# A GRU network and graph attention: the last three pairs get an attention schedule of their own

## The chip, the cores and the metric

The kernel runs on one core of a Trainium2 chip. Its time is device microseconds of one execution; each kernel is run several times and the median is given. A core has TensorE (PE, matrix products and transposes into PSUM), VectorE (DVE), ScalarE (ACT, table functions and copies), GpSimd (POOL) and SyncE (SP), which issues the transfers here. The engines run side by side, each works through its own instructions in order, and semaphores tie them together.

## The reference

There are 64 graphs with 256 nodes and 256 features. Layer 0 is three rounds of a gated recurrent unit (GRU) over the adjacency matrix, layer 1 is graph attention; each adds its input and normalises.

```python
def gru(inp, h):
    gi, gh = inp @ w_ih.T + b_ih, h @ w_hh.T + b_hh        # 3 parts each: r, z, n
    r, z = sigmoid(i_r + h_r), sigmoid(i_z + h_z)
    n = tanh(i_n + r * h_n)
    return (1 - z) * n + z * h
h = x
for i in range(3):
    m = h @ weight[i]
    h = gru(einsum('bst,bsd->btd', adj != 0, m), h)
v = layernorm(x + h)
Wh = v @ W;  s1, s2 = Wh @ a[:256], Wh @ a[256:]
e = leaky_relu(s1[:, :, None] + s2[:, None, :], 0.2)
attn = softmax(where(adj > 0, e, -9e15), axis=2)
out = layernorm(v + attn @ Wh)
```

## The kernel before

The graphs are worked off in 32 pairs (`NP`), numbered 0 to 31. A pair has four blocks of 128 nodes (`K`), two to a graph (`C`). A GRU round of a pair is a *block* `(p, i)`, pair and layer. The blocks go in diagonals, so that three pairs are under way at a time: (p, 0), (p-1, 1), (p-2, 2). The list therefore ends with (29,2), (31,1), (30,2), (31,2), each a GRU round, and after a pair's third round comes its attention.

The order of the work is written out by hand. A clock counts *ticks*; `at(t, step)` puts a step on a heap, and `tick()` inside a block's products (line 468 and 473) runs the steps that are due. A block has 12 ticks. What a step issues stands, on every engine's queue, behind all that was issued before it. When the blocks are all issued, the loop of line 788 runs the remaining steps in the order of their ticks, with no products between them.

A GRU round keeps its state transposed, `hT` (features on partitions, 512 nodes of the pair on the free axis). A 32-bit product is built of three pieces of each operand, `hH`, `hL`, `hD` and `aH`, `aL`, `aD` (line 465). PE writes banks of PSUM, ACT and DVE empty them (lines 470 to 474), ACT computes sigmoid and tanh (483), POOL multiplies and adds (491 to 501), DVE forms the new `hT` (504).

Attention of pair p, whose clock starts at t, the end of its third block (`attention`, line 543), in the kernel before, by ticks from t:

- +7, +13: x, transposed, comes back from DRAM (`vT <- xT`, line 550), and `hT` is added to it.
- +24, +29, +32: v is turned to node-major order by the DMA's transpose, which works on 16-bit halves: two transposes (line 296), four gathers (302), and on ACT four copies that join the halves (286).
- +34, +36: statistics of the first layer norm (DVE), power (POOL).
- +37 to +41: projection with W and both score vectors (PE, line 586), scaling (595, 597); the adjacency matrix is loaded again and made into a mask (622).
- +42 to +47: score rows turned by PE (605), leaky scores (ACT, 609), masking (DVE, 628), maxima (630), exponentials with their sums (ACT, 633).
- +50 to +57: the weights are turned: for pairs 0 to 29 by two DMA transposes, eight gathers and four joins (655, 302, 670), for pairs 30 and 31 by PE and a DVE copy (648, 701).
- +58 (+54 for the last two) on: combination `po` (PE, 680), division and residual (DVE, 691), second layer norm (DVE, POOL, and ACT in line 531), store (706).

With T for the tick at which block (29,2) ends, the three last blocks take T to T+12, to T+24 and to T+36; pair 29 has t = T, pair 30 t = T+24, pair 31 t = T+36.

`room` (line 264) says where the tiles of attention lie: pairs 0 to 29 in a pool of their own (`late`), 30 and 31 in buffers of the GRU pieces, which are free by then.

Of the kernel before, what the change touches and what calls it, by code (L numbers as in the profile page):

```python
# [9 lines left out]
F32 = mybir.dt.float32  # L10
F32R = mybir.dt.float32r
U8 = mybir.dt.uint8
# [15 lines left out]
def kernel(  # L28
# [37 lines left out]
    nc = tc.nc  # L66
    B, N, D = x.shape
    L = weight.shape[0]
    C = N // P
    G = 2  # L70
# [18 lines left out]
    def at(t, step):  # L89
        clock[1] += 1  # L90
        heappush(pending, (t, clock[1], step))
# [14 lines left out]
    def bank(name):  # L106
        return psum.tile([P, 512], F32, tag="bank", name=name)
# [255 lines left out]
    def from_T(hT, d):  # L363
        pt = bank("pt")
        for k in range(K):
            nc.tensor.transpose(pt[:, k * P:(k + 1) * P], hT[:, d, k * P:(k + 1) * P], ident)  # L366
        return pt
# [174 lines left out]

    def attention(p, t):
# [97 lines left out]
            nc.vector.reciprocal(s.sm, s.sm)  # L641
        at(t + 51, divide)

        def weights_T(g):
            pts[g] = bank("pt")
            for j in range(C):
                for c in range(C):
                    nc.tensor.transpose(pts[g][:, (j * C + c) * P:(j * C + c + 1) * P],
                                        s.sc[:, g * C + c, j * P:(j + 1) * P], ident)
# [13 lines left out]
        def gather_weights(g):  # L663
            gather(planes(g), s.eT[:, g].rearrange("p c j n -> p (c j n)").bitcast(U16).rearrange(
                "p (m b n) -> p m b n", b=2, n=P))

        def join_weights(g):
            dst = s.eT[:, g].rearrange("p c j n -> p (c j n)").bitcast(U16).rearrange("p (n h) -> p h n", h=2)
            for h in (1, 0):
                ENGINES[("aa", "aa")[g][1 - h]](dst[:, h], planes(g)[:, h].rearrange("p m n -> p (m n)"))  # L670

        def combine(g):
            pts[g] = bank("po")
            for c in range(C):
                for j in range(C):
                    if by_dma:
                        e = s.eT[:, g, c, j, :]
                    else:
                        e = s.sc[:, g * C + j, c * P:(c + 1) * P]
                    nc.tensor.matmul(pts[g][:, c * D:(c + 1) * D], e, s.wh[:, g, j, :],  # L680
                                     start=(j == 0), stop=(j == C - 1))

        def add(g):

            if by_dma:
                s.o = s.eT.rearrange("p g c j n -> p g c (j n)")
            else:
                s.o = s.v
            for c in range(C):
                k = g * C + c  # L690
                nc.vector.scalar_tensor_tensor(s.o[:, g, c, :], pts[g][:, c * D:(c + 1) * D], s.sm[:, k:k + 1],
                                               s.v[:, g, c, :], op0=ALU.mult, op1=ALU.add)
        by_dma = p < NP - 2
        for g in range(G):
            if by_dma:
# [3 lines left out]
            else:  # L699
                at(t + 51 + g, lambda g=g: weights_T(g))  # L700
                at(t + 52 + g, lambda g=g: nc.vector.tensor_copy(flat(s.sc[:, g * C:(g + 1) * C, :]), pts[g]))
            at(t + (58 if by_dma else 54) + g, lambda g=g: combine(g))
            at(t + (58 if by_dma else 54) + 1 + g, lambda g=g: add(g))
# [4 lines left out]
        at(t + 60, lambda: layer_norm(s.o, f"b_{p}", (t + 60 + 1, t + 64, t + 66, t + 71), s.eps, store))  # L708


    CLOSE = (5, 5, 5, 7, 8, 8), (6, 6, 7)
# [50 lines left out]
    for n, (p, i) in enumerate(blocks):  # L762
        if n + 1 < len(blocks):
            np_, ni = blocks[n + 1]
            if ni == 0:
                if np_ < FROM:
                    after(1, lambda p=np_: begin(p))
                after(1, lambda p=np_: take_x(p))
                after(2, lambda p=np_: ones(p))
                nxt = np_ + 1  # L770
                if nxt < FROM:
                    after(7, lambda p=nxt: load_x(p))
                elif nxt < NP:
                    later = {}
                    after(26, lambda p=nxt, d=later: d.update(f=x_turned(p)))
                    after(30, lambda d=later: d["f"]())
                    after(33, lambda p=nxt: x_joined(p))
                    after(33, lambda p=nxt: load_x(p))
                after(5 if nxt < FROM else 34, lambda p=nxt: load_adj(p))
            front(np_, ni, clock[0],   # L780
                  CLOSE if n and np_ == blocks[n - 1][0] else
                  EARLY if np_ < FROM and not ni else (FIRST, SECOND, THIRD)[ni])
        gates(p, i, (2, 3, 5) if n + 2 >= len(blocks) or blocks[n + 2][0] == p else (2, 5, 9))
        if i == L - 1:
            attention(p, clock[0])
        elif FROM <= p and p + i + 1 < NP:
            h_turned(p, i, clock[0])
    while pending:
# [31 lines left out]
```

## Time and profile before

| | us |
|---|---|
| median of 3 runs (2116.19 to 2118.03) | 2117.34 |
| the profiled execution | 2112.89 |
| its span (first to last instruction) | 2111.1 |
| PE busy | 2053.3 (97%) |
| DVE, ACT, POOL busy | 1769.4, 1659.1, 1611.8 |
| mean granted clock of PE | 0.988 |

The page has a table of busy time by engine, the span in 40 slices, the transfers, the chain of work that ended last (followed back from the last instruction to whatever released each step) and the groups of instructions. Beside it the trace can be asked for the busy time of each engine in any stretch, and for each engine's instructions in order, with the idle time ahead of each and what ended it. The start of one instruction to the start of the next is what it costs on its engine; the durations given overlap by some 0.1 us on DVE and ACT, and on PE by more.

### The profile page before, as it was taken

Reading aid. Unit: us, or ns where it says so; the run is one execution under the profiler, and the core shown is the slowest. Engines: PE = TensorE matmul, PEld = TensorE weight load, DVE = VectorE, ACT = ScalarE, POOL = GpSimd, SP = SyncE. Lnnn points to the kernel's source line nnn. Section 1 sums busy time; section 2 is a strip of 40 time slices with the busy share of each in tenths; the row PEclk is TensorE's granted clock in tenths of the full one; section 3 lists DMA queues with packets and bytes.
Section 4 is the critical chain, followed back from the end, with each engine's and each line's share of the span. In section 5 each row is a group of like instructions: output and inputs, shape, how many; then the busy total and the mean of one; then the engine's idle time right before and its main releaser. Section 6 shows DMA issues by size and latency. Waiting matters only on the chain.

```text
span 2111.1 us, 31355 instructions
## 1 busy us (share of the span) xinstructions
PE 2053.3 (97%) x9860; PEld 1726.3 (82%) x9860; DVE 1769.4 (84%) x2863; ACT 1659.1 (79%) x3020; POOL 1611.8 (76%) x1114
## 2 busy tenths in 40 slices
PE   8999999999999999999999999999999999999965
PEld 5788888888888888888888888888888888888854
DVE  5666778899898899998899989888999889998765
ACT  4566788788888888888888888888888888888754
POOL 6778677777787887787888778788778788877641
PEclk9999999999999999999999999999999999999987
DMA  4111234666566666566666566666656656654333
GB/s 130 31 41 41 71 89 111 150 131 127 133 140 136 144 126 145 124 134 139 133 150 130 128 132 140 133 148 121 151 122 135 138 134 150 130 129 92 71 88 82
DMA packets 545509, 252.17 MB, mean 119 GB/s; under 512 B 370432, under 2 KB 537088, under 8 KB 545344
## 3 DMA queue, kind: packets, MB, share of 16 engines
q1 hardware_dynamic: 543552, 248.34, 53.2%
q8 instruction: 78, 1.28, 0.3%
q10 hardware_dynamic: 1616, 1.57, 0.2%
q14 instruction: 87, 0.71, 0.1%
q0 software_dynamic: 176, 0.27, 0.1%
HBM read 69.74 MB, written 33.55 MB: 49 GB/s over the span
## 4 chain that ended last, share of the span: by engine, by line
PE 93%; DVE 2%; POOL 2%; DMA 1%; ACT 1%; SPq 1%; issue 0%; POOLq 0%; ACTq 0%; DVEq 0%
PE pga L465 48%; PE pgb L465 24%; PE pa L436 8%; PE po L680 5%; PE pwh L586 5%; PE s L605 1%; PE pt L366 1%; SPq L302 1%; DMA rows_hH<-in_L_gnn_w_hh_dram 0%; DMA v<-vT 0%; POOL t L491 0%; POOL n L501 0%; DMA second<-v 0%; POOL t L492 0%; PE pw L238 0%
## 5 line engine op out<-in xcount | busy, mean ns | idle before, releaser
L491 POOL TENSOR_TENSOR t<-hT,n 128x512 f32<-128x512 f32 x192 | 264.2, 1376 | 186.2 <-ACT n L483 186.0
L501 POOL TENSOR_TENSOR n<-n,t 128x512 f32<-128x512 f32 x192 | 287.4, 1497 | 117.8 <-DVE t L474 113.7
L497 POOL TENSOR_TENSOR n<-n,r 128x512 f32<-128x512 f32 x192 | 316.1, 1646 | 73.6 <-ACT r L483 48.5
L465 PE MATMUL pga<-hH,whhH_whh 128*128 128x512 f32 x1152 | 370.6, 403 | 0.0
L465 PE MATMUL pgb<-hD,whhD_whh 128*128 128x512 f32 x1152 | 357.1, 391 | 1.4 <-DVE hD L138 1.4
L465 PE MATMUL pga<-hL,whhL_whh 128*128 128x512 f32 x1152 | 356.8, 391 | 0.3 <-POOL hL L135 0.3
L492 POOL TENSOR_TENSOR t<-t,z 128x512 f32<-128x512 f32 x192 | 271.0, 1411 | 15.0
L135 POOL TENSOR_TENSOR hL<-hT,hH 128x1024 fp32r<-128x1024 f32 x96 | 258.3, 2691 | 10.6 <-ACT hH L132 10.5
L465 PEld LDWEIGHTS pgb<-hD,whhD_whh 128*128 128x128 f32 x1152 | 216.2, 188 | 49.1 <-DVE hD L138 1.7
L465 PEld LDWEIGHTS pga<-hL,whhL_whh 128*128 128x128 f32 x1152 | 216.4, 188 | 47.8 <-POOL hL L135 0.8
L465 PEld LDWEIGHTS pga<-hH,whhH_whh 128*128 128x128 f32 x1152 | 207.9, 189 | 34.3
L138 DVE SCALAR_TENSOR_TENSOR hD<-hH,hT 128x1024 fp32r<-128x1024 f32 x96 | 202.4, 2109 | 0.0
L470 ACT ACTIVATE r<-pga 128x512 f32<-128x512 f32 x192 | 114.0, 594 | 109.1 <-PE pga L465 75.9
L483 ACT ACTIVATE n<-n,bi 128x512 f32<-128x512 f32 x192 | 138.9, 723 | 75.5 <-POOL n L501 75.4
L436 PE MATMUL pa<-A,hi 128*128 128x256 f32 x768 | 193.6, 285 | 0.2 <-DVE A L377 0.2
L504 DVE TENSOR_TENSOR hT<-t,n 128x512 f32<-128x512 f32 x192 | 187.6, 977 | 5.9 <-POOL t L492 5.9
L436 PE MATMUL pa<-A,lo 128*128 128x256 f32 x768 | 192.1, 283 | 0.0
L474 DVE SCALAR_TENSOR_TENSOR r<-pgb,r 128x512 f32<-128x512 f32 x192 | 132.0, 688 | 69.0 <-PE pgb L465 44.3
L135 DVE TENSOR_TENSOR aL<-pa,aH 128x512 fp32r<-128x512 f32 x192 | 131.1, 683 | 63.8 <-ACT aH L132 63.7
L132 ACT ACTIVATE aH<-pa 128x512 fp32r<-128x512 f32 x192 | 115.9, 604 | 64.0 <-PE pa L436 64.0
L470 ACT ACTIVATE t<-pga 128x512 f32<-128x512 f32 x192 | 115.3, 601 | 59.2 <-PE pga L465 54.3
L483 ACT ACTIVATE z<-z,b_sum 128x512 f32<-128x512 f32 x192 | 140.7, 733 | 18.9 <-DVE z L474 18.1
(147 smaller groups left out, 5391.1 us busy)
## 6 DMA issues: line engine op xcount, KB each, us to landing
adj<-in_adj_dram SPq DMA_DIRECT2D x64, 512.0 KB, 3.8
second_h<-first_h SPq DMA_DIRECT2D x204, 128.0 KB, 4.0
x<-in_x_dram SPq DMA_DIRECT2D x32, 512.0 KB, 3.8
xT<-hT SPq DMA_DIRECT2D x32, 512.0 KB, 4.5
vT<-xT SPq DMA_DIRECT2D x32, 512.0 KB, 3.3
second<-v SPq DMA_DIRECT2D x128, 128.0 KB, 3.6
sc<-eT SPq DMA_DIRECT2D x240, 64.0 KB, 2.2
out_dram<-eT SPq DMA_DIRECT2D x30, 512.0 KB, 4.3
```

The lines of the kernel that those rows point to most:

```text
L135: eng.tensor_sub(dst, src, hi.bitcast(F32))
L138: nc.vector.scalar_tensor_tensor(dst, hi.bitcast(F32), 1.0 + U, src, op0=ALU.mult, op1=ALU.subtract)
L436: nc.tensor.matmul(pt[:, g * N:(g + 1) * N], h[:, g * C + c, :], s.A[:, g, c, :], start=(n == 0), stop=(n == len(todo) - 1))
L465: nc.tensor.matmul(pt, w[:, d, o * P:(o + 1) * P], m[:, d, :], start=n in (0, ends + 1), stop=n in (ends, len(todo) - 1))
L470: nc.scalar.activation(dst, a, AF.Copy, scale=1.0 + U)
L474: nc.vector.scalar_tensor_tensor(dst, b, -1.0 / U, dst, op0=ALU.mult, op1=ALU.add)
L483: nc.scalar.activation(dst, dst, func, bias=bias)
L491: nc.gpsimd.tensor_sub(t, h, n)
L492: nc.gpsimd.tensor_mul(t, t, z)
L497: after(2, lambda r=r, n=n: nc.gpsimd.tensor_mul(n, n, r))
L501: after(1, lambda n=n, t=t: nc.gpsimd.tensor_add(n, n, t))
L504: after(lags[2], lambda n=n, t=t, h=h: nc.vector.tensor_add(h, t, n))
```

## The change

The last three pairs, 29 to 31, get a function of their own, `attention_last`. In it v and the weights are turned by PE (transposes into PSUM, then copies by ACT and DVE); masks, masking, maxima, exponentials, division and the steps after them are made graph by graph; the addition to `vT` is split in two; scaling goes to ACT for odd node blocks and to DVE for even ones (before: first two ACT, last two DVE). Each of the three pairs has a timetable (`LAST`, ticks from its t), with shorter distances than before. Tiles of pair 29 move, `vT` apart: v to the place of x, wh to that of A, the weights to that of hT. The path of the last two pairs in `attention` goes away.

```diff
-        if p < NP - 2:
+        if p < NP - 3 or p == NP - 3 and kind == "vT":
             return late.tile(shape, F32, tag=kind, name=name, bufs=2 if kind == "v" else 1)
+        if p == NP - 3:
+            pool, tag, bufs = {"v": (io, "x", 1), "wh": (work, "A", 3), "sc": (work, "hT", 4)}[kind]
+            return pool.tile(shape, F32, tag=tag, name=name, bufs=bufs)
         tag = {"v": "hH", "vT": "hD", "wh": "aH", "sc": "aD"}[kind]
...
-        by_dma = p < NP - 2
         for g in range(G):
-            if by_dma:
-                at(t + 50 + g, lambda g=g: turn_weights(g))
-                at(t + 52 + g, lambda g=g: gather_weights(g))
-                at(t + 56 + g, lambda g=g: join_weights(g))
-            else:
-                at(t + 51 + g, lambda g=g: weights_T(g))
-                at(t + 52 + g, lambda g=g: nc.vector.tensor_copy(flat(s.sc[:, g * C:(g + 1) * C, :]), pts[g]))
...
+    def attention_last(p, t, T):
+        s = pairs[p]
+        pts = {}
+        each = lambda step, dt, every=1, n=G: [at(t + dt + every * g, lambda g=g: step(g)) for g in range(n)]
...
+        def sum_(d):
+            nc.vector.tensor_add(s.vT[:, d, :], s.vT[:, d, :], s.hT[:, d, :])
+
+        def turn(d):
+            if d == 0:
+                s.v = room("v", [P, G, C, D], p)
+            pts["v", d] = from_T(s.vT, d)
+
+        def turned(d):
+            evacuate(nodes(s.v, d), pts["v", d].rearrange("p (k n) -> p k n", k=K))
...
+        def spread(k):
+            rs = s.rs[:, k:k + 1]
+            for dst, src in ((s.s1[:, k:k + 1], pts[k][:, D:D + 1]),
+                             (s.s2[:, k, :], pts[k][:, D + 1:D + 2].to_broadcast([P, P])),
+                             (s.wh[:, k // C, k % C, :], pts[k][:, :D])):
+                if k % 2:
+                    nc.scalar.activation(dst, src, AF.Copy, scale=rs)
+                else:
+                    nc.vector.tensor_scalar(dst, src, rs, None, op0=ALU.mult)
+
+        def rows(g):
+            pts["s2", g] = bank("s2")
+            for c in range(C):
+                nc.tensor.transpose(pts["s2", g][:, c * P:(c + 1) * P], s.s2[:, g * C + c, :], ident)
...
+        def exps(g):
+            for k in range(g * C, (g + 1) * C):
+                nc.scalar.activation(s.sc[:, k, :], s.sc[:, k, :], AF.Exp, bias=s.nm[:, k:k + 1],
+                                     accum_out=s.sm[:, k:k + 1])
...
+        def weights_T(g):
+            pts["w", g] = bank("pt")
+            for j in range(C):
+                for c in range(C):
+                    nc.tensor.transpose(pts["w", g][:, (j * C + c) * P:(j * C + c + 1) * P],
+                                        s.sc[:, g * C + c, j * P:(j + 1) * P], ident)
+
+        def weights(g):
+            for j in range(C):
+                nc_copy = ENGINES["av"[j]]
+                nc_copy(s.sc[:, g * C + j, :], pts["w", g][:, j * N:(j + 1) * N])
...
+        at(t + T["again"], again)
+        each(sum_, T["add"])
+        at(t + T["adja"], adj_again)
+        each(turn, T["turn"])
+        each(turned, T["turn"] + 1)
+        at(t + T["st"], norm)
+        each(project, T["proj"], 1, K)
+        each(spread, T["spr"], 1, K)
+        each(rows, T["rows"], T["e_rows"])
+        each(mask, T["mask"], T["e_mask"])
+        each(scores, T["sco"], T["e_sco"])
+        each(masked, T["mskd"], T["e_mskd"])
+        each(top, T["max"], T["e_max"])
+        each(exps, T["exp"], T["e_exp"])
+        each(divide, T["div"], 1)
+        each(weights_T, T["wT"], T["e_wT"])
+        each(weights, T["wc"], T["e_wc"])
+        each(combine, T["comb"], T["e_comb"])
+        each(add, T["res"], T["e_res"])
+        at(t + T["l2"], norm_last)
...
+    LAST = (
+        dict(again=5, add=10, adja=8, turn=13, st=15, pw=17, proj=17, spr=19, rows=22, mask=18, sco=22, mskd=24, max=27, exp=28, div=30, wT=30, wc=30, comb=31, res=32, l2=32, l2p=34, l2s=37, l2a=39, e_rows=1, e_mask=1, e_sco=1, e_mskd=1, e_max=1, e_exp=1, e_wT=1, e_wc=1, e_comb=1, e_res=1),
+        dict(again=5, add=9, adja=8, turn=12, st=15, pw=17, proj=12, spr=20, rows=22, mask=16, sco=22, mskd=24, max=24, exp=26, div=28, wT=27, wc=28, comb=30, res=31, l2=31, l2p=34, l2s=35, l2a=38, e_rows=1, e_mask=1, e_sco=1, e_mskd=1, e_max=1, e_exp=1, e_wT=1, e_wc=1, e_comb=1, e_res=1),
+        dict(again=4, add=6, adja=11, turn=6, st=10, pw=12, proj=9, spr=15, rows=17, mask=15, sco=17, mskd=18, max=19, exp=21, div=22, wT=21, wc=22, comb=24, res=25, l2=25, l2p=28, l2s=29, l2a=31, e_rows=1, e_mask=1, e_sco=1, e_mskd=1, e_max=1, e_exp=1, e_wT=1, e_wc=1, e_comb=1, e_res=1),
+    )
...
         if i == L - 1:
-            attention(p, clock[0])
+            if p < NP - len(LAST):
+                attention(p, clock[0])
+            else:
+                attention_last(p, clock[0], LAST[p - NP])
```

The steps that are left out here (`again`, `norm`, `project`, `scores`, `mask`, `masked`, `top`, `divide`, `combine`, `add`, `store`) issue what their namesakes in `attention` issue, for one graph or one node block at a time.

More of the change, by code (lines that the diff above doesn't have):

```diff
@@ L642, in attention @@
         at(t + 51, divide)
[L644 to L649, printed above, removed]
         def turn_weights(g):
@@ L675, in combine @@
                 for j in range(C):
-                    if by_dma:
-                        e = s.eT[:, g, c, j, :]
-                    else:
-                        e = s.sc[:, g * C + j, c * P:(c + 1) * P]
+                    e = s.eT[:, g, c, j, :]
                     nc.tensor.matmul(pts[g][:, c * D:(c + 1) * D], e, s.wh[:, g, j, :],
@@ L683, in add @@
         def add(g):
[L685 to L688, printed above, removed]
+            s.o = s.eT.rearrange("p g c j n -> p g c (j n)")
             for c in range(C):
@@ L692, in add @@
                                                s.v[:, g, c, :], op0=ALU.mult, op1=ALU.add)
-        by_dma = p < NP - 2
         for g in range(G):
-            if by_dma:
-                at(t + 50 + g, lambda g=g: turn_weights(g))
-                at(t + 52 + g, lambda g=g: gather_weights(g))
-                at(t + 56 + g, lambda g=g: join_weights(g))
-            else:
-                at(t + 51 + g, lambda g=g: weights_T(g))
-                at(t + 52 + g, lambda g=g: nc.vector.tensor_copy(flat(s.sc[:, g * C:(g + 1) * C, :]), pts[g]))
-            at(t + (58 if by_dma else 54) + g, lambda g=g: combine(g))
-            at(t + (58 if by_dma else 54) + 1 + g, lambda g=g: add(g))
+            at(t + 50 + g, lambda g=g: turn_weights(g))
+            at(t + 52 + g, lambda g=g: gather_weights(g))
+            at(t + 56 + g, lambda g=g: join_weights(g))
+            at(t + 58 + g, lambda g=g: combine(g))
+            at(t + 59 + g, lambda g=g: add(g))
         def store():
@@ L708, in attention, with again, norm, adj_again @@
         at(t + 60, lambda: layer_norm(s.o, f"b_{p}", (t + 60 + 1, t + 64, t + 66, t + 71), s.eps, store))
+    def attention_last(p, t, T):
+        s = pairs[p]
+        pts = {}
+        each = lambda step, dt, every=1, n=G: [at(t + dt + every * g, lambda g=g: step(g)) for g in range(n)]
+        def again():
+            s.vT = room("vT", [P, C, GN], p)
+            nc.sync.dma_start(s.vT, s.far)
+        def sum_(d):
[6 more added lines that the diff above has]
+            evacuate(nodes(s.v, d), pts["v", d].rearrange("p (k n) -> p k n", k=K))
+        def norm():
+            s.rs, s.eps = layer_norm(s.v, f"a_{p}", (t + T["st"], t + T["pw"]))
+        def adj_again():
+            load_adj(p)
+        def project(k):
+            if k == 0:
+                s.wh = room("wh", [P, G, C, D], p)
+                s.sc = room("sc", [P, K, N], p)
+                s.s1 = work.tile([P, K], F32, tag="s1", name=f"s1_{p}")
+                s.s2 = s.sc[:, :, :P]
+                s.nm = work.tile([P, K], F32, tag="nm", name=f"nm_{p}")
+                s.sm = work.tile([P, K], F32, tag="sm", name=f"sm_{p}")
+            pts[k] = bank("pwh")
+            for d in range(C):
+                nc.tensor.matmul(pts[k][:, :D + 2], s.vT[:, d, k * P:(k + 1) * P], gw[:, d, :],
+                                 start=(d == 0), stop=(d == C - 1))
+        def spread(k):
[11 more added lines that the diff above has]
+                nc.tensor.transpose(pts["s2", g][:, c * P:(c + 1) * P], s.s2[:, g * C + c, :], ident)
+        def scores(g):
+            for k in range(g * C, (g + 1) * C):
+                nc.scalar.activation(s.sc[:, k, :], pts["s2", g][:, :N], AF.Prelu,
+                                     bias=s.s1[:, k:k + 1], alpha=ALPHA)
+        def mask(g):
+            if g == 0:
+                s.adj = loaded_adj.pop(p).rearrange("p g c n -> p g (c n)")
+                s.mask = work.tile([P, K, N], U8, tag="mask", name=f"mask_{p}", bufs=1)
+            nc.vector.tensor_scalar(flat(s.mask[:, g * C:(g + 1) * C, :]), s.adj[:, g], 0.0, None, op0=ALU.is_le)
+        def masked(g):
+            ks = slice(g * C, (g + 1) * C)
+            nc.vector.copy_predicated(flat(s.sc[:, ks, :]), flat(s.mask[:, ks, :]), neg.to_broadcast([P, C * N]))
+        def top(g):
+            ks = slice(g * C, (g + 1) * C)
+            nc.vector.tensor_reduce(s.nm[:, ks], s.sc[:, ks, :], AX.X, ALU.max, negate=True)
+        def exps(g):
+            for k in range(g * C, (g + 1) * C):
+                nc.scalar.activation(s.sc[:, k, :], s.sc[:, k, :], AF.Exp, bias=s.nm[:, k:k + 1],
+                                     accum_out=s.sm[:, k:k + 1])
+        def divide(g):
+            ks = slice(g * C, (g + 1) * C)
+            nc.vector.tensor_mul(s.sm[:, ks], s.sm[:, ks], s.rs[:, ks])
+            nc.vector.reciprocal(s.sm[:, ks], s.sm[:, ks])
+        def weights_T(g):
[8 more added lines that the diff above has]
+                nc_copy(s.sc[:, g * C + j, :], pts["w", g][:, j * N:(j + 1) * N])
+        def combine(g):
+            pts["o", g] = bank("po")
+            for c in range(C):
+                for j in range(C):
+                    nc.tensor.matmul(pts["o", g][:, c * D:(c + 1) * D], s.sc[:, g * C + j, c * P:(c + 1) * P],
+                                     s.wh[:, g, j, :], start=(j == 0), stop=(j == C - 1))
+        def add(g):
+            for c in range(C):
+                k = g * C + c
+                nc.vector.scalar_tensor_tensor(s.v[:, g, c, :], pts["o", g][:, c * D:(c + 1) * D],
+                                               s.sm[:, k:k + 1], s.v[:, g, c, :], op0=ALU.mult, op1=ALU.add)
+        def norm_last():
+            layer_norm(s.v, f"b_{p}", (t + T["l2"], t + T["l2p"], t + T["l2s"], t + T["l2a"]), s.eps, store)
+        def store():
+            nc.sync.dma_start(out[p * G:(p + 1) * G].rearrange("g (c p) d -> p g c d", p=P), s.v)
+        at(t + T["again"], again)
[18 more added lines that the diff above has]
+        at(t + T["l2"], norm_last)
```

## The prediction

> **What bounds the kernel now.** I read the page's table by engine first: TensorE (PE) is busy for 97% of the span, so until its matmuls end, time is PE's. Then the 40 slices: only the last three differ. The busy time by stretch separates the last blocks from what follows (after the stretch and its length: PE, its weight loads, VectorE (DVE), ScalarE (ACT), GpSimd (POOL), granted clock, DMA share, GB/s):
>
> ```profile
> 1970.50:1993.70 23.20, 23.20 (x117) 19.59 (x116) 18.12 (x33) 18.26 (x38) 17.65 (x14) 1.00 0.13 46
> 1993.70:2018.00 24.30, 22.95 (x114) 19.18 (x113) 17.87 (x24) 16.82 (x30) 14.46 (x9) 1.00 0.21 44
> 2018.00:2034.40 16.40, 16.40 (x74) 13.57 (x73) 10.60 (x24) 10.79 (x18) 10.52 (x9) 1.00 0.58 129
> ...
> 2040.00:2060.00 20.00, 0.91 (x4) 0.50 (x3) 6.42 (x12) 6.42 (x17) 3.34 (x3) 0.53 0.49 102
> ```
>
> The three first rows are the blocks (31,1), (30,2), (31,2) (pair, GRU layer), in which PE works all the time; DVE leaves 63.9 - 46.6 = 17.3 us free there, ACT 18.0. The last product ends at 2034.5. Call this moment G. From G to the end at 2111.1 are 76.6 us, a tail that holds the attention of pairs 29, 30 and 31. The chain that ended last says what it waits for:
>
> ```profile
> 2049.98 3.28 DMA eT<-sc
> ...
> 2061.67 1.35 SPq L296
> 2063.70 4.62 DMA v<-vT
> 2070.51 3.45 DMA second<-v
> ...
> 2093.88 6.37 PE po L680 x16
> ```
>
> So pair 29's softmax weights go through a DMA transpose, then pair 31's v, behind it in SP's queue, through another, and the pairs follow each other. The same in PE's timeline (in brackets its idle time and what ended it):
>
> ```profile
> 2003.86 0.66 PE L366 MATMUL pt<-ident,hT 128*128 128x128 f32 x4 [1.35 <-DVE hT L504]
> ...
> 2062.03 3.50 PE L680 MATMUL po<-wh,eT 128*128 128x256 f32 x8 [19.16 <-ACT eT L670]
> 2066.79 1.99 PE L680 MATMUL po<-wh,eT 128*128 128x256 f32 x8 [1.26 <-ACT eT L670]
> ...
> 2083.19 1.89 PE L680 MATMUL po<-wh,sc 128*128 128x256 f32 x8
> ...
> 2093.88 6.35 PE L680 MATMUL po<-wh,sc 128*128 128x256 f32 x16
> ```
>
> PE waits 19.16 us for pair 29's weights, and once, 1.35 us, inside the GRU work.
>
> **The change, 1: pair 29 moves ahead of G.** T is the tick at which block (29,2) ends (1970.5); blocks have 12 ticks, so G is T+36. Before, pair 29's transposes start at T+24 and its projection is in the tail. After, v is turned at T+13, projected from T+17, masked at T+24, exponentiated at T+28, weights turned at T+30, combined at T+31, all ahead of G. PE's price for such work inside a block is read from starts in its timeline:
>
> ```profile
> 1944.97 1.89 PE L680 MATMUL po<-wh,eT 128*128 128x256 f32 x8
> 1946.51 0.81 PE L465 MATMUL pga<-aL,wc1L_wc 128*128 128x512 f32 x2
> 1947.16 0.63 PE L465 MATMUL pgb<-hD,whhD_whh 128*128 128x512 f32 x2
> ```
>
> A half of combine takes 1.54 to the next start, which itself runs 0.20 longer than the usual 0.455: 1.74, twice is 3.5. By the same reading (starts at 1908.49, 1909.17, 1909.82; 1953.95, 1954.30, 1954.85) projection is 4 x 0.89 = 3.5 and four transposes are 0.45: v 0.9, score rows 0.5, weights 0.9. Sum 9.3 us. Four transposes of v and two of the projections (2.7 us in all) come before the hT transpose that waited 1.35 us, and fill that wait. Net 8.0.
>
> New waits on PE: score rows, weights and combine come in two graphs each, six places where GRU products queue behind a wait for DVE or ACT that started one or two ticks earlier (a tick is 1.4 to 2.0 us here). DVE gets some 11 us more in these blocks (sum 1.2, copy 0.6, statistics 2.1, scaling 1.6, mask and masking 2.1, maxima 1.2, division and copies 1.4, result 1.6, second statistics 2.1, less statistics and sum that were there before), ACT some 9 less 2.8 of joins. Their 17.3 and 18.0 free us, and the 8 by which the stretch grows, cover that; the waits in detail may not. From below 0, since PE's waits for the same steps of earlier pairs in these blocks were 0 (with leads of several ticks); from above 6 x 5.3 = 32, if each stands for a whole chain (maximum 0.6, table 1.28, exponentials 2.0, transposes 0.5, copies 0.9). I take 2 us in all, nearer to the first, the row of the same steps between the same products. **G moves by +10.0, to 2044.5.**
>
> ACT must switch its table to exponentials and back inside block (31,2), which it did not for pair 29 before. The row:
>
> ```profile
> 1991.18 1.28 ACT L633 ACT_TABLE_LOAD   x1
> 1992.47 0.51 ACT L633 ACTIVATE sc<-sc,nm 128x256 f32<-128x256 f32 x1
> ...
> 1995.53 1.28 ACT L483 ACT_TABLE_LOAD   x1
> 1996.83 0.73 ACT L483 ACTIVATE z<-z,b_sum 128x512 f32<-128x512 f32 x1
> ```
>
> By the row a switch is 1.3 us from start to start, two are 2.6. The Trainium skill (ScalarE: Activation LUTs, "What ACT_TABLE_LOAD costs") gives about 2.66 us each, a drain after the load included: 5.3. The next activation starts 0.01 us after the load here, so I take the row. By the row the switches lie in ACT's free time; by the rule 2.7 us more would stand ahead of pair 29's copies, which PE awaits (G 2047.2).
>
> **2: pairs 30 and 31 without transfers.** SP issues 8 DMA transposes and 20 gathers less (pair 29: 2+2 and 4+8; the others 2 and 4 each), 8 transposes of v per pair go to PE instead (0.9). What remains on SP is hidden: adj of pair 29 now goes ahead of pair 28's weights transposes, due six ticks later, and waits only for a mask due at T+5. vT of pair 31 needs the last hD, read some 1.4 us before G; it takes 4.5, lands by G+3.1, and its sum starts at G+7.0. Behind it wait pair 29's store (its scaling ends near G+6) and adj of 31, landing by G+11.5 for a mask near G+16. Cover 4 us; late, it would hold DVE as long.
>
> **3: the new tail**, laid out engine by engine in the new order from the durations in the trace (half-sized masking 0.7, maximum 0.6, mask 0.38 are estimates from rows of 1.38, 1.14 and 0.60 between starts), 0.06 per handover. What sets the end, from G:
> - last gate of pair 31: evictions to G+1.65, add 1.3, tanh 0.72, difference 1.35, product 1.3, sum 0.68: G+7.0. (Before, 10.6: the same chain stood behind pair 29's statistics and joins.)
> - two additions 1.2, PE turns 0.5: G+8.7.
> - DVE then scales two tiles of pair 30 (1.56), copies (0.6), takes statistics of 31 (2.1): G+12.4; masks and maxima of 30, 2.6: G+15.0.
> - exponentials of 30 (second graph) 1.0, transposes 0.5: G+16.7. Copies, PE combines 30 with the score rows of 31 between: G+19.6 for the rows, scores of 31 to G+20.5.
> - DVE: masking and maxima of 31 among 30's residual and statistics: G+24.3.
> - exponentials 1.0, transposes 0.5, copies: combine of 31 starts at G+26.1.
> - combine, both graphs: 3.5 at full clock, 6.4 at half.
> - residual 0.8, two statistics 1.06, POOL's power 1.46 and shift, scaling 2.07, from there to the end 4.1 as before.
>
> That is G+39.4 at full clock and G+42.3 at half. The last row of PE's timeline above is that combine at half clock, after PE had been idle or at transposes alone since 2087.2:
>
> ```profile
> 2044.00:2046.00 2.00, 0.00 (x0) 0.00 (x0) 1.72 (x2) 0.54 (x2) 0.25 (x1) 0.50 0.04 5
> 2096.00:2098.00 2.00, 2.00 (x6) 1.55 (x6) 0.30 (x1) 0.70 (x2) 0.00 (x0) 0.50 0.16 57
> ```
>
> (The figure after POOL's is the clock.) The Trainium skill (TensorE: Matmul & The Clock Gate, Part 1) says that an idle window of about 3.4 us halves the clock and one as long of sustained work restores it. Here the half clock outlasted 6 us of work, 2092.8 to 2099.4. In the new tail PE has only eight transposes from G+21.4 to G+26.1, so I take half clock to the end; by the rule a restoration halfway would give G+41.
>
> **Sum.** 2044.5 + 42.3 = 2086.8, against a span of 2111.1: -24.3. That profiled execution took 2112.9; the median of the runs, 2117.34, is 6.2 above the span. 2086.8 + 6.2 = **2093.0**, 1.1% faster.
>
> **Rivals.**
> - *Smoother* (0.20): all waits on PE covered (-2), clock full in the last combine (-2.9): 2088. For it: ACT and DVE have more room in these blocks than earlier, where PE never waits. Against it: the cold combine of before.
> - *The pairs in series* (0.20): DVE becomes the bound of the tail and its order chains 30 to 31. In the old tail pair 30 took 18 us from its first power (2069.3) to the end of its combine (2087.2), pair 31 23.0 from its masking to the end. With 12 ahead of both, 53 after G: 2044.5 + 53 + 6.2 = 2104. For it: DVE has 23 us of work left after hT in my layout, and PE's order puts rows of 31 behind the weights of 30. Against it: the orders do interleave.
> - *Transfers hidden anyway* (0.03): gates and DVE set the tail as much, nothing within 4 us of 2117 is gained. Against it: during the 19.16 us PE and DVE have nothing else.
> - *Slower* (0.04): GRU products queue behind pair 29's six waits. The mechanism decides from (24.3 + 2) / 6 = 4.4 us each, and is slower by over 0.2% from 5.1; at the whole chain's 5.3 it gives 2093 - 2 + 32 = 2123. For it: PE waited 3.3 and 4.2 us for exponentials in the old tail. Against it: there it had nothing ahead of them, here a tick or two of products.
>
> **How the numbers follow.** My forecast has 0.53, with its own range 2089 to 2099. The range 2086 to 2105 takes in the smoother end and the serial one, and leaves out the tails of these (0.1) and the last two. Changes within 0.2% (4.2 us) cannot be told from none here: faster 0.93, same 0.03, slower 0.04.
>
> **What would show it.** Last product near 2044.5 and no idle of PE over 2 us before it; two table loads around T+28 in block (31,2); no DMA transpose after pair 28's weights; last hT at G+7, last combine from G+26 over 6.4 us at clock 0.5; end 42 after G. The forecast is wrong if products wait behind pair 29's transposes or combine, if hT of 31 comes later than G+11, or if score rows of 31 wait for all of pair 30.

## The result, and the profile after

The changed kernel took 2093.0 us (median of 4 runs, 2090.9 to 2094.3) against 2116.8 for the kernel before on the same chip (2116.2 to 2118.0): a ratio of 0.9886, interval 0.9869 to 0.9903. The profiled execution took 2091.9 with a span of 2090.0, 21.1 less than the span before.

The busy time by stretch of the changed kernel (after the stretch and its length: PE, its weight loads, DVE, ACT, POOL, granted clock, DMA share, GB/s). The first three rows are again the blocks (31,1), (30,2), (31,2), the fourth is the tail:

```profile
1976.42:1999.62 23.20, 23.20 (x118) 19.58 (x116) 18.11 (x33) 18.26 (x38) 17.85 (x14) 1.00 0.21 69
1999.62:2023.92 24.30, 24.30 (x126) 20.62 (x125) 20.97 (x40) 19.12 (x38) 13.93 (x13) 1.00 0.21 44
2023.92:2048.00 24.08, 24.08 (x114) 20.12 (x113) 20.22 (x48) 16.01 (x32) 13.54 (x13) 1.00 0.13 45
2048.00:2090.00 42.00, 23.76 (x105) 18.09 (x103) 28.77 (x86) 23.17 (x60) 10.66 (x14) 0.86 0.23 75
```

PE is now without a gap to the last product. From there to the end are 42.0 us, where there were 76.6. Its timeline, from pair 29's weights on:

```profile
2035.36 0.60 PE L784 MATMUL pt<-ident,sc 128*128 128x128 f32 x4
...
2037.62 1.89 PE L796 MATMUL po<-wh,sc 128*128 128x256 f32 x8
...
2055.52 1.21 PE L369 MATMUL pt<-ident,vT 128*128 128x128 f32 x8 [3.05 <-DVE vT L707]
...
2065.90 2.77 PE L796 MATMUL po<-wh,sc 128*128 128x256 f32 x8
...
2074.33 1.40 PE L784 MATMUL pt<-ident,sc 128*128 128x128 f32 x4 [1.45 <-ACT sc L772]
2075.51 4.80 PE L796 MATMUL po<-wh,sc 128*128 128x256 f32 x16
```

The wait of 19.16 us for weights turned by DMA is gone. The longest wait of the tail is 3.05, for pair 31's sums, and those stand behind its last `hT`.

**Where the two traces part.** The two profiled executions differ before the change begins. The first half of pair 27's combine, which is the same work in both kernels, starts at 1944.97 before and at 1950.89 after. I measure from this point, *the reference*. G is taken here at the start of the instruction after the last product, some 0.15 before the end that the trace models for it.

| us from the reference | before | after | difference |
|---|---|---|---|
| last product (G) | 89.4 | 97.1 | +7.7 |
| end of span | 166.1 | 139.1 | -27.0 |
| so the tail, G to end | 76.7 | 42.0 | -34.7 |

Between these two executions the change is worth 27.0 us, and 5.9 of it were lost ahead of the reference. The loss is at a meeting of DVE and POOL that comes once per group of three blocks (62.4 us). Two such places in the timelines of the changed kernel, with the product on PE that waits at the first:

```profile
1256.17 2.93 DVE L135 TENSOR_TENSOR lo<-V,hi 128x512 fp32r<-128x512 f32 x1
1256.17 2.38 POOL L135 TENSOR_TENSOR hL<-hT,hH 128x1024 fp32r<-128x1024 f32 x1
1259.15 0.39 PE L439 MATMUL pa<-A,lo 128*128 128x256 f32 x1 [1.22 <-DVE lo L135]
...
1320.02 0.68 DVE L135 TENSOR_TENSOR lo<-V,hi 128x512 fp32r<-128x512 f32 x1
1320.02 2.94 POOL L135 TENSOR_TENSOR hL<-hT,hH 128x1024 fp32r<-128x1024 f32 x1
```

DVE's `lo` of the third layer and POOL's `hL` start in the same hundredth of a microsecond. If POOL wins, `lo` takes 2.93 instead of 0.68, PE waits 1.22 for it, and the group takes 1.5 us more. Such a meeting I call a tie, and lost where DVE comes second. The execution profiled before lost 0 of 25 ties, the one after lost 5, and takes 7.5 us more from pair 0's combine to the reference. The start-up, which varies, gives 1.6 of that back: pair 0's combine starts at 257.7 before and 256.1 after.

### The profile page after: what moved, and what is told of

The parts are those of the page before. It is cut to its first block, busy times and chain, and to the rows that moved or that the text cites. A ratio compares the mean times of both kernels' runs of the same rounds, so it can differ in the third digit from the quotient of the medians.

```text
span 2090.0 us, 31381 instructions
## 1 busy us (share of the span) xinstructions
PE 2052.3 (98%) x9892; PEld 1726.0 (83%) x9892; DVE 1780.5 (85%) x2886; ACT 1655.3 (79%) x3015; POOL 1604.8 (77%) x1114
## 4 chain that ended last, share of the span: by engine, by line
PE 89%; DVE 3%; ACT 3%; issue 2%; POOL 1%; DMA 1%; SPq 0%; POOLq 0%; ACTq 0%; DVEq 0%
PE pga L468 46%; PE pgb L468 23%; PE pa L439 8%; PE pwh L589 5%; PE po L673 5%; DVE lo L135 1%; PE s L608 1%; PE pt L369 1%; ACT sc L636 1%; DMA rows_hH<-in_L_gnn_w_hh_dram 0%; PE po L796 0%; ACT L636 0%; PE pw L238 0%; ACT n L475 0%; DMA second<-v 0%
## 5 line engine op out<-in xcount | busy, mean ns | idle before, releaser
L504 POOL TENSOR_TENSOR n<-n,t 128x512 f32<-128x512 f32 x192 | 282.7, 1472 | 122.7 <-DVE t L477 116.0
L138 DVE SCALAR_TENSOR_TENSOR hD<-hH,hT 128x1024 fp32r<-128x1024 f32 x96 | 195.7, 2039 | 0.0
L486 ACT ACTIVATE n<-n,bi 128x512 f32<-128x512 f32 x192 | 139.1, 724 | 64.0 <-POOL n L504 63.8
L439 PEld LDWEIGHTS pa<-A,lo 128*128 128x128 f32 x768 | 146.4, 191 | 13.8 <-DVE lo L135 7.6
```

The costliest lines, as they stand in the source:

```text
L138: nc.vector.scalar_tensor_tensor(dst, hi.bitcast(F32), 1.0 + U, src, op0=ALU.mult, op1=ALU.subtract)
L439: nc.tensor.matmul(pt[:, g * N:(g + 1) * N], h[:, g * C + c, :], s.A[:, g, c, :], start=(n == 0), stop=(n == len(todo) - 1))
L486: nc.scalar.activation(dst, dst, func, bias=bias)
L504: after(1, lambda n=n, t=t: nc.gpsimd.tensor_add(n, n, t))
```

## The experiments

Times "from the reference" leave the ties out: in four executions of the changed kernel G repeats within 0.1 us, and the end lies between 138.3 and 139.8. Medians carry the ties.

**The changed kernel again.** Nothing edited.

> The changed kernel once more, unaltered. In its first trace DVE's lo<-V took 2.93 us in place of 0.68 in 5 of 25 periods, each time with a wait of 1.22 us on PE; the kernel before had none in its trace. Theory (a tie): lo and POOL's hL start within 0.01 us of each other in every period, and chance decides who goes first, so the count differs here from 5 and the time moves by about 1.5 us for each. Rival (the change moved something that makes it lose): 5 again at the same periods. From the last combine of pair 27 to the end 139.1 us in both, since no tie lies there.

Measured: 2087.6 (2085.6 to 2090.7), ratio 0.9862 (0.9847 to 0.9877). Profiled: two lost ties, G at 97.1 and the end at 139.8 from the reference. The count of lost ties differs with nothing edited, so it is not the change that loses them.

**The kernel before again.**

> The kernel before once more, unaltered, for the same tie: its first trace had no lo above 1 us, and that execution was 3.3 to 5.1 us shorter than the runs. Theory (tie by chance): two to four long lo in this trace if its time is near 2116. Rival (it never loses the tie): none, and a time that differs for another reason.

Measured: 2114.5 in the one run, with 2 lost ties; G at 89.4, end at 164.6. The kernel before has the tie too, and the profile I predicted from happened to lose none. Over the executions of both kernels, from pair 0's combine to the reference, 1687.2 and 1687.4 us pass with no tie lost, 1688.8 with one, 1690.3 and 1690.4 with two, 1694.8 with five: 1.5 us for each.

The end is 1.5 earlier than in the first profile, because the last combine takes 4.75 here and 6.35 there. Against this execution the change is worth 25.5 us from the reference. The 27.0 used below is against the first, so parts of 1 or 2 us are within what repeats differ by.

**Pair 29 left as it was, pairs 30 and 31 new.** Their timetables are 8 ticks later, since the buffers of pair 29's old attention are free only then; small tiles get a third buffer and the mask another place. Pair 29's timetable falls away.

```diff
-        if p < NP - 3 or p == NP - 3 and kind == "vT":
+        if p < NP - 2:
...
-                attention_last(p, clock[0], LAST[p - NP])
+                attention_last(p, clock[0], {k: v if k[:2] == "e_" else v + 8 for k, v in LAST[p - NP].items()})
```

> Pair 29 keeps the attention of before (DMA transposes, its old ticks); pairs 30 and 31 have the new one, 8 ticks later than in the change, so that the three fit into the small buffers. Theory W (the transfers of 30 and 31 behind those of 29 made the tail; where pair 29 lies is minor): G as before, tail some 52 us, from pair 27's last combine to the end 141.5 us (166.1 before, 139.1 changed), about 2% of the tail's gain lost. Theory P (taking pair 29 out of the tail is the gain, a third of its work): at most a third of the 27 us is kept, 157 us.

Measured: 2096.8, ratio 0.9907 (0.9892 to 0.9922). G at 89.3, as before; tail 59.1; end at 148.4. 17.7 of the 27.0 us stay, between both expectations. With pair 29 in the tail, its weights by DMA cost PE only 3.0 us of waiting, but the tail is 17.1 longer than with pair 29 ahead of G (the 8 ticks by which the others stand later included), for 7.8 saved before G.

**Pair 29 new, pairs 30 and 31 as they were,** with the branches for them (`by_dma`) back in the old attention.

```diff
-            if p < NP - len(LAST):
+            if p != NP - 3:
                 attention(p, clock[0])
             else:
                 attention_last(p, clock[0], LAST[p - NP])
...
+        by_dma = p < NP - 2
```

> Only pair 29 has the new attention and timetable; 30 and 31 keep the one of before, v turned by DMA. Theory W: G 8 us later as in the change, then two rounds of DMA transposes and gathers on the path, tail 56 us: 153.5 us from pair 27's last combine to the end, a gain of 12.6 of the 27. Theory P: two thirds of the gain, 148 us or less.

Measured: 2113.0 (2108.0 to 2118.6), ratio 0.9986 (0.9975 to 0.9996). End at 163.1: only 3.0 of the 27.0 us stay, less than either expectation. The chain of this kernel says why:

```profile
2050.97 1.98 ACT v L534 x4
...
2054.05 1.80 SPq L299
2055.90 4.43 DMA v<-vT
...
2062.37 3.43 DMA second<-v
```

Pair 29 no longer sends anything through the DMA transposes. But its store, which waits for its scaling (the first row), stands in SP's queue ahead of the transposes of the next v, and then transpose and gather take their time as before; PE waits 19.1 us for the score rows behind them. The transfers of pairs 30 and 31 were hidden behind pair 29's, and its removal uncovers them.

**All three turned by PE, but at the old places.** The timetables are moved back so that v is turned at the tick where it was before, +24. The reload of x and the sum come later than they did: at +16 to +22 instead of +7, and at +21 to +24 instead of +13.

```diff
-                attention_last(p, clock[0], LAST[p - NP])
+                late_by = (11, 12, 18)[p - NP + 3]
+                attention_last(p, clock[0], {k: v if k[:2] == "e_" else v + late_by for k, v in LAST[p - NP].items()})
```

> All three pairs turn v and weights by PE as in the change, but their timetables start where the old ones did (v turned at +24: later by 11, 12 and 18 ticks), so that pair 29's scores, exponentials and combination fall behind G. Theory W: the transfers are gone all the same; G moves by some 3 us in place of 8, tail about 49: 141.5 us from pair 27's last combine to the end. Theory P: pair 29 is back in the tail and most of the gain goes, 150 us or more.

Measured: 2108.9, ratio 0.9960 (0.9944 to 0.9975). End at 158.8. With no DMA transpose left, 7.3 of 27.0 us are gained. My expectation from the transfers alone missed by 17 us, because it left the order of DVE's queue out. DVE's timeline in this kernel:

```profile
2050.71 0.84 DVE L802 SCALAR_TENSOR_TENSOR v<-po,sm,v 128x256 f32<-128x256 f32 x2
...
2052.55 1.26 DVE L707 TENSOR_TENSOR vT<-vT,hT 128x512 f32<-128x512 f32 x2
...
2079.17 0.39 DVE L518 BATCH_NORM_STATS2 st_b<-v 128x6 f32<-128x256 f32 x1
...
2079.69 0.19 DVE L744 TENSOR_SCALAR s<-pwh,rs_a 128x1 f32<-128x1 f32 x1
```

Pair 30's sum (2052.55) stands behind pair 29's residual (2050.71) and its statistics, though it needs neither; pair 31's scaling (2079.69) behind the last statistics of pair 30. The last combine starts at 2088.6, 50 us after G. The late reload and sum belong to this timetable, so the run does not show what the old order alone would give without transfers. On the chip where these three ran, the medians agree with the traces: 18.9, 2.8 and 6.9 us for the parts, 28.1 for the whole change. None of the parts carries the gain: the transfers have to go, and the places have to move so that the queues do not put the pairs in series.

**Pair 29 without its lead.** Division, weights, copies and combine at the tick of the exponentials, where the changed kernel has two and three ticks between.

```diff
-        dict(again=5, add=10, adja=8, turn=13, st=15, pw=17, proj=17, spr=19, rows=22, mask=18, sco=22, mskd=24, max=27, exp=28, div=30, wT=30, wc=30, comb=31, res=32, l2=32, l2p=34, l2s=37, l2a=39, e_rows=1, e_mask=1, e_sco=1, e_mskd=1, e_max=1, e_exp=1, e_wT=1, e_wc=1, e_comb=1, e_res=1),
+        dict(again=5, add=10, adja=8, turn=13, st=15, pw=17, proj=17, spr=19, rows=22, mask=18, sco=22, mskd=24, max=27, exp=28, div=28, wT=28, wc=28, comb=28, res=32, l2=32, l2p=34, l2s=37, l2a=39, e_rows=1, e_mask=1, e_sco=1, e_mskd=1, e_max=1, e_exp=1, e_wT=1, e_wc=1, e_comb=1, e_res=1),
```

> Pair 29's transposes of the weights, copies and combination are put in the ticks of its exponentials (T+28 and T+29 in place of T+30 to T+32), so that PE meets them with no products ahead. Theory (a wait on PE ahead of G costs its full length, and one tick of lead hides a chain of this kind): PE waits some 2.5 us for the first graph and 2.2 for the second, G 4.7 later, from pair 27's last combine to the end 143.8 in place of 139.1. Rival of the forecast (each such place costs the whole chain of 5.3): two graphs with two waits each, 10 to 21 us more. Second rival (the tail takes it up, since pair 29 ends earlier): 139 to 140.

Measured: 2094.8, ratio 0.9898 (0.9883 to 0.9912); G at 103.1, end at 145.5. G is 6.0 later than in the changed kernel, 1.3 more than expected. PE waits 2.95 of it in the trace. The clock explains more than half of the rest (same columns as in the first table of stretches):

```profile
2030.00:2032.00 2.00, 1.48 (x6) 1.18 (x6) 0.89 (x3) 0.37 (x1) 0.31 (x1) 0.85 0.01 4
2032.00:2034.00 2.00, 2.00 (x6) 1.57 (x5) 0.00 (x0) 0.00 (x0) 0.00 (x0) 0.50 0.00 0
```

After waits of 1.59, 0.16 and 0.52 us with a few transposes between, the clock falls to one half; the first combine then takes 3.02 instead of 1.89, and the products behind it are slower until 2035. From start to start the combine and the two products after it take 4.4 instead of 2.7, 1.8 of the 3.1 that remain. The lead of two and three ticks is what kept these four of the six new waits at nothing; the score rows kept their lead in this run.

**A warm tail.** Transposes of the identity that nobody reads keep PE busy where it waited; the work that counts is the same.

```diff
+        def fill(n):
+            pt = bank("fill")
+            for k in range(n):
+                nc.tensor.transpose(pt[:, k % 4 * P:(k % 4 + 1) * P], ident, ident)
+        if p > NP - 3:
+            if p == NP - 1:
+                at(t + T["turn"] - .5, lambda: fill(30))
+            at(t + T["wT"] - .5, lambda: fill(14 if p == NP - 2 else 12))
+            at(t + T["wT"] + .5, lambda: fill(4 if p == NP - 2 else 14))
```

> The changed kernel with PE's idle places in the tail filled by transposes of the identity that nobody reads (30, 14, 4, 12 and 14, at 0.09 us each, no longer than the idle time that the trace shows there), so that its clock is not halved. Theory (half clock costs part of the tail: the transposes of 30 and 31 took 1.18 for 0.43 between starts, the first combine of 30 2.6 for 1.74, the last combine 4.8 for 3.5): clock 1.00 through the tail, last combine 3.5 us, from pair 27's last combine to the end 136.6 us in place of 139.1. Rival (DVE is the bound of the tail, the PE steps have slack): the combine is shorter, the end moves by less than 1 us.

Measured: 2085.7 (2084.4 to 2088.8), ratio 0.9855 (0.9841 to 0.9870); G at 97.1, end at 136.5, no lost tie in the profile. The end of PE's timeline, and the stretch from G to the end of PE's work (the figure after POOL's is the clock):

```profile
2066.74 1.69 PE L831 MATMUL fill<-ident 128*128 128x128 f32 x14
...
2069.24 3.62 PE L796 MATMUL po<-wh,sc 128*128 128x256 f32 x16
...
2043.10:2073.00 29.90, 28.72 (x179) 23.96 (x177) 26.64 (x79) 20.94 (x56) 9.54 (x12) 1.00 0.23 71
```

The last combine takes 3.62 instead of 4.80 and starts 26.1 after G instead of 27.6; the tail is 39.4. Its end from the reference is 2.6 us ahead of the changed kernel's 139.1, and 1.8 ahead of the earliest of four, 138.3. It is the best version of this study by that measure. The medians of this run cannot prove it: 2085.7 is also the median of one repetition of the changed kernel, below.

**The tie, first try.** `hL` one tick later.

```diff
-    THIRD = (2, 3, 4, 7, 8, 9), (3, 6, 7)
+    THIRD = (2, 3, 4, 7, 8, 9), (3, 7, 7)
```

> The changed kernel with hL of a pair's third round issued one tick later (7 in place of 6), behind the sum that POOL makes for the other pair, so that it no longer starts with DVE's lo. Theory (tie): no lo above 1 us, no wait of PE on it, less spread between runs, and a median lower by 1.5 us times the ties lost, 2 to 5 of them: 3 to 7 us against the changed kernel, ratio to the kernel before 0.983 to 0.985. Rival (the collision only moves to the next pair of instructions): the same waits elsewhere and a ratio of 0.986 to 0.989 as measured for the change.

Measured: 2089.4 (2085.8 to 2091.5), ratio 0.9874 (0.9858 to 0.9891); G 97.1, end 139.1. The experiment says nothing for or against: the edit left the order on every engine as it was, `lo` and `hL` both start at 1253.12 in its trace, and that the profile shows no lost tie is chance. It counts as the changed kernel once more.

**The tie, second try,** beside the changed kernel a third time. `hL` is put ahead of POOL's `n<-n,r`.

```diff
-    THIRD = (2, 3, 4, 7, 8, 9), (3, 6, 7)
+    THIRD = (2, 3, 4, 7, 8, 9), (3, 5, 7)
```

> The changed kernel a third time, beside the next two on the same chip. If what differs between executions is mainly the tie (VectorE's lo and GpSimd's hL starting within 0.01 us) and a start-up that varies by 1.3 us: profiled time = 2085.6 without a lost tie, and 1.45 more for each; runs from 2085 to 2094. From the reference combine to the last GRU product 97.1, to the end 139.1, as in every execution of it so far.

> hL of the third layer stands ahead of n<-n,r in GpSimd's order (in e6_no_tie the order of no engine had changed: that edit was the changed kernel again, and lo and hL still start at the same hundredth there). hL then runs from 1254.7 to 1257.2 on the clock of the profile after, with lo due at 1256.2. Theory (the tie makes the spread): lo always waits for hL's end and ends near 1257.8, 0.1 before TensorE needs it, so no lost ties at 2.9 us, no TensorE wait over 0.3 us, runs within 2 us of each other at 2085.5, 1.5 to 3 us under the changed kernel's median of the same call. Rival: lo ends later than 1257.9 or n, 1.5 us later, reaches the hT chain: a wait of 0.3 us or more on TensorE in each of 25 periods, 8 us or more slower than the changed kernel.

> e8_hL_before_n and the fillers of e4_warm_clock together (transposes of the identity that nobody reads keep TensorE busy in the tail; the result is untouched). Theory: both add up, from the reference combine to the end 136.5, 2083 in the median with a spread of 2 us, 1.5 to 3 us under e4's 2085.7. Rival, as in e8_hL_before_n: a wait in each period, slower than the changed kernel.

| | median (range) | ratio (interval) | from the reference: G, end | 
|---|---|---|---|
| changed, third time | 2085.7 (2085.0 to 2087.2) | 0.9861 (0.9846 to 0.9876) | 97.1, 138.3 |
| `hL` before `n` | 2092.1 (2091.2 to 2093.8) | 0.9893 (0.9876 to 0.9909) | 97.1, 140.4 |
| the same with fillers | 2089.7 (2087.4 to 2090.0) | 0.9877 (0.9862 to 0.9891) | 97.1, 136.5 |

DVE and POOL in the kernel with `hL` before `n`:

```profile
1254.83 1.70 DVE L135 TENSOR_TENSOR lo<-V,hi 128x512 fp32r<-128x512 f32 x1
...
1253.39 2.59 POOL L135 TENSOR_TENSOR hL<-hT,hH 128x1024 fp32r<-128x1024 f32 x1
```

The tie is gone: `lo` takes 1.69 to 1.71 in all 25 places. As expected it waits for `hL` each time, and the runs of each of the two kernels lie within 2.6 us, where the 16 of the changed kernel range over 9.3. The price was wrong. Between the product with `hi` and the one behind it, which reads `lo`, 0.26 us pass where 0.12 is usual, and the group takes 62.61 instead of 62.37; 0.24 times 25 is 6.0 us, as much as four lost ties. That the tie makes the spread agrees with this, on four runs of each kernel; a set of the changed kernel alone can be as narrow (2.3). The hope of a faster kernel fell, and the rival's 8 us were not reached. What the medians of these two kernels do show is the gain of the fillers: with no tie in either, 2089.7 stands against 2092.1, and their runs do not overlap.

## Why the prediction was right, and where by luck

**The sum.** I predicted 24.3 us less, from two steps: G 10.0 later, the tail 34.3 shorter. Measured from the reference: G 7.7 later, the tail 34.7 shorter, 27.0 in all (25.5 against the second execution of the kernel before). All executions of the changed kernel put together (the four sets above) have a median of 2089.1 in 16 runs, those of the kernel before 2115.9 in 34: 26.8 less. The predicted 2093.0 is the first set's median to the tenth, which is luck: its profile lost 5 ties, and the other three sets have medians of 2085.7 to 2089.4. Over all sets I was 2.5 us short of the gain.

- **G.** Work of 9.3 less the filled stall of 1.35 makes 8.0; measured 7.7. (In the 2.7 us that fill the stall, "four transposes of v" should be eight, 0.9; the sum is right.) The combine of pair 29 takes 1.73 in the chain, where I had 1.74. The stall before the hT transpose is gone. *The term that was mis-sized is the 2 us for six new waits: they cost nothing.* Runs and trace show why for four of them: they were issued two to three ticks after what they need, and when that lead is taken away they cost 6.0. This was the half of the rival "smoother" that came true. The rival "slower" is excluded by G itself, and even without lead those four places cost 6.0, where it needed 26 from six.
- **ACT's table.** The row decided, and it decided rightly:

```profile
2032.44 1.28 ACT L772 ACT_TABLE_LOAD   x1
2033.73 0.51 ACT L772 ACTIVATE sc<-sc,nm 128x256 f32<-128x256 f32 x1
...
2038.27 1.28 ACT L486 ACT_TABLE_LOAD   x1
2039.57 0.73 ACT L486 ACTIVATE z<-z,b_sum 128x512 f32<-128x512 f32 x1
```

  The next activation starts 0.01 and 0.02 us after the load ends, and PE shows no gap in this block. The 2.66 us of the Trainium skill (ScalarE: Activation LUTs, "What ACT_TABLE_LOAD costs"), a drain included, are not seen here.
- **SP's queue.** No transpose or gather follows pair 28's weights. What remains is hidden, as said, but of the cover of 4 us only 0.5 was left, and that is luck:

```profile
2048.18 1.08 ACT L534 ACTIVATE eT<-eT,nmr_b,rs_b 128x256 f32<-128x256 f32 x2
...
2049.28 0.38 SPq L691 DMA_DIRECT2D out_dram<-eT  x1
2049.76 0.45 SPq L704 DMA_DIRECT2D vT<-xT  x1
...
2054.74 1.28 DVE L707 TENSOR_TENSOR vT<-vT,hT 128x512 f32<-128x512 f32 x2
```

  The store of pair 28 stands ahead of pair 31's x in SP's queue and waits for its scaling on ACT. The prediction left it out. So x is issued at G+1.8 and lands 4.4 later, at G+6.3 instead of G+3.1, and the sum starts at G+6.8, directly behind `hT`.
- **The tail's start.** The last `hT` ends at G+6.9 (predicted 7.0), PE's turn of the sums at G+8.6 (8.7). The chain of the gates had indeed been held by pair 29's statistics and joins in the old tail.
- **The tail's middle and end.** Maxima of 30 at G+15.5 (15.0), weights of 30 at G+17.5 (16.7), scores of 31 at G+21.8 (20.5), maxima of 31 at G+25.6 (24.3), last combine at G+27.6 (26.1), end at 42.0 (42.3). The end is right and the way to it is not. I put the whole price of the half clock, 2.9, into the last combine. It took 4.80, so 1.2 over its 3.6 at full clock; pair 30's first combine took 2.77 instead of 1.89 and four transposes of weights 1.2 at half clock (start to start) instead of 0.45, and from there the last combine comes 1.5 late. 1.2 + 1.5 = 2.7 against 2.9. With fillers the landmarks are those of my layout at full clock: last combine at G+26.1, end at G+39.4, both to the tenth.
- **The clock's rule.** I had taken the row (half clock outlasted 6 us of work) over the rule of the Trainium skill (TensorE: Matmul & The Clock Gate, Part 1: restored after about 3.4 us of sustained work). In the last combine the rule was the better guide: granted 0.62 and 0.53 in the stretches 2074 to 2076 and 2076 to 2078, 1.00 from 2078. In the three other executions of this tail that combine took 4.78, 4.93 and 5.12, never 6.4. My row was an exception in its own kernel too. The same tail in the first and in the second execution of the kernel before:

```profile
2092.42:2095.83 3.41, 3.31 (x10) 2.25 (x10) 2.03 (x7) 1.62 (x5) 1.23 (x2) 0.50 0.00 0
2095.83:2099.25 3.42, 3.42 (x10) 2.70 (x9) 0.88 (x2) 0.87 (x2) 0.00 (x0) 0.50 0.44 153
...
2095.81:2099.22 3.41, 3.18 (x9) 2.26 (x9) 1.86 (x7) 1.62 (x5) 1.23 (x2) 0.50 0.00 0
2099.22:2101.90 2.68, 2.64 (x12) 1.98 (x11) 0.88 (x3) 0.72 (x2) 0.00 (x0) 1.00 0.37 128
```

  In all 13 traces each half-clock stretch after the first 20 us that ends within the kernel's work lasts 3.41 us or a whole multiple of it (up to 23.89), and those at the end of one execution begin whole multiples of 3.41 apart (2041.22, 2078.77, 2092.42 in the first). Call these steps windows. Wherever, after 1900 us, PE was busy for 2.75 us or more of a window at half clock, the clock was full in the next, but for one: the first row above. Why that one was not enough stays open.
- **Pairs in series.** This rival (tail of 53) is far from the changed kernel (42). It describes, by its kind and not its size, the run with the old places (65). What it got right is the danger: the orders of DVE and PE, not their busy time, decide.
- **Median against span.** I added 6.2, the median of before less the span of its profile. About 1.8 of it lies around the span. The rest is most likely ties, of which that profile lost none, at 1.5 us each; the runs without a trace do not show their count. It was right to carry it over, but by luck, since I did not know what it was: the changed kernel has the same tie.

## What to carry to other kernels

When several waits hide behind one another in in-order queues, removing one uncovers the next: here parts gave 17.7, 3.0 and 7.3 us where the whole gave 27.0, so cost the last wait that remains and walk each queue in its new order. Moving work under a busy engine cost its busy time and no more here, since each step is issued some ticks after what it needs; with the lead taken away the same steps stalled, and the clock fell behind the stalls. Follow each queue back to what it stands behind, stores of earlier pairs included. Compare traces from an event that both kernels share and that lies ahead of the change, before reading a microsecond of difference as the change's.

## What was not expected of the hardware

Two instructions that start at the same time on DVE and POOL, each reading two operands from SBUF, are served one after the other here, in an order that changes from execution to execution: 0 to 5 of 25 lost by DVE, 2.93 or 0.68 us for it, 2.38 or 2.94 for POOL. The Trainium skill (SBUF — State Buffer, "SBUF: two separate sides") describes a port pair that the two engines lock for a whole instruction; the durations agree with it, as the one that comes second takes about as long as both together. In a schedule that repeats every 62.4 us such a tie repeats too, and here it moves the time by up to 7 us.

The clock does not follow the length of a single wait. In the run without lead PE has 1.74 us of work in the window from 2027.98 to 2031.39 and no wait over 1.59, and the clock is halved behind it, in the midst of a busy block. In the changed kernel two windows from 2050.60 to 2057.42 hold 1.87 and 1.90 us of work and a wait of 3.05, and it stays full. Busy time alone does not part the cases either: in the first repetition of the changed kernel a window with 1.94 us of work was followed by half clock.
